# Moving the prologue and the last feed-forward of a two-layer sequence model: x first, tile 0 first, another order of steps

## The chip, the cores and the metric

One NeuronCore of a Trainium2 chip (trn2) runs the whole program in one launch. The metric is the device time in microseconds; lower is better. Engines are named as in the profile: PE (matrix products; PEld its weight loads), DVE (vector engine), ACT (activation functions), POOL (GpSimd) and SP (it issues most of the transfers). Every number is f32.

## The reference

The input x has 16 sequences of 512 tokens of 256 channels. Two layers follow each other, each an attention-like part and a feed-forward part, with a layer norm (LN, no weights) after each residual sum.

```
x = LN(x + attention(x))        # 16 heads of 16; q, k, v are taken on to 32 latents a head, rotary
                                # positions on q and k, a further matrix on q, causal softmax
x = LN(x + ffn(x))              # gate, up: 256 -> 704, down: 704 -> 256; silu(gate) * up;
                                # inputs AND weights of all three quantized to FP4 in blocks of 16
x = LN(x + recurrence(x))       # 16 heads with 64 states:
                                #   state[t] = tanh(state[t-1] @ tanh(a) + xnorm[t] @ b)
                                #   out[t] = state[t] @ c + skip * xnorm[t];   512 steps in order
x = LN(x + r * ((relu(k)**2) @ Wv))   # r = sigmoid(xr @ Wr), k = xk @ Wk; xr and xk mix each token
                                      # with the one before it
```

FP4 quantization takes the largest magnitude of each block of 16, scales by it and rounds to a grid of eight magnitudes. It needs a whole row of its input, and for the down projection a whole row of `h = silu(gate) * up`.

## The kernel before, in words

The program has two stages that follow each other. The first does layer 0 for one sequence after another; the second does layer 1 for all sequences at once, one time step after another. Between them layer 0's output goes to a DRAM tile `xs`, ordered by time and then by sequence.

**Prologue (lines 139 to 256).** Constants and weights are loaded on the queues of SP and ACT. The attention weights `caw` (768 KB) are transposed into `wqk`; the value, latent and output matrices are multiplied into each other (`there`, `wv`) and their biases into `bo`, which is added to the residual x. Only then do the pools for x open, and `load(0)` (line 709) asks for sequence 0's transposed x, `xT`. Then `heads`, `values` and the three steps of `latents` for head group 0 run, and the first scores can begin.

**Layer 0, main loop (lines 713 to 752).** A sequence has 4 groups of 4 heads, and each group has three slots (row blocks 3, 2, and 1 with 0). In a slot `scores` multiplies q and k (L551) into four PSUM banks, DVE adds the mask and takes the maximum (L563), `exponentials` runs on ACT (L576) two heads behind, and one slot later `turn` transposes the weights on PE (L586) and ACT copies them out (L588). After a group `weighted` multiplies by the values (L617), and `divide` divides by the sums (L638). Each slot is cut into 8 half slots. In a half slot the class `Beside` takes further steps from a list, so many that its planned times (`TIME`) are spread evenly over the sequence. The list is `PLAN`: a letter for the task, the sequence relative to the present one, and the tile or group. `H` are head products (L383), four steps; `V` values (L366); `L` latents, three steps (L401 with DVE at L411; L401, L416 and POOL at L417; L420 and ACT at L422); `O` the output projection with residual and LN (L435 to L448); `Q` starts a quantization; `U` gate and up (L483, L493), three steps; `D` down (L514, L524), two steps; `W` the feed-forward weights, 30 steps, in sequence 0 alone. So the feed-forward of sequence b runs beside the attention of b + 1 and b + 2. The order of PE is exactly the order in which the program is written down. A scheduler orders the other engines' queues. Quantizations (`fp4`, L290 to L304: eight operations on DVE, two on POOL) are cut into pieces, and `vector_step` writes down one piece in each half slot. PSUM has eight banks: one for `py`, seven that `mm` hands out. After the last sequence, `rest` runs what is left of the lists (lines 749 to 752): the output projection and the whole feed-forward of sequence 15, and the leftover tiles of sequence 14.

**Layer 1 (lines 755 to 1102).** Time step t multiplies the state (L988, `advance_state`), adds inputs that `inputs` (L950) has put into the PSUM tile `u` in groups of eight steps, and applies tanh on ACT (L996). Two halves of the heads alternate. Beside them run, in macro steps of 16 time steps, the tasks of layer 1's remaining work: `N` loads and RMS-normalizes tokens and transposes them (`normed`, L785 to L802), `R` reads the states out (L966), `A` is the product with `w_out`, `M` the token mixing, `K`, `G`, `V` the last feed-forward. `product` (L830) computes each of these products in two halves of 64 output columns. Two PSUM banks serve these tasks, three serve `u`. Macro step p needs the tokens 16p to 16p + 15 of all sequences, so the first eight need only tile 0 (tokens 0 to 127) of each.

Of the kernel before, what the change touches and what calls it, by code (L numbers as in the profile page):

```python
# [57 lines left out]
def tile_kernel(ctx: ExitStack, tc: tile.TileContext, I: dict, out: bass.AP):  # L58
# [79 lines left out]

    with ExitStack() as a:
        wts = a.enter_context(tc.tile_pool(name="wts", bufs=1))  # L140

# [23 lines left out]
        bd = {}  # L165
        for k in ("bdq", "bdk", "bdks"):
            bd[k] = wts.tile([P, 256], F32, name=k)
            nc.scalar.dma_start(bd[k], I[k])
# [14 lines left out]
        wgT = wts.tile([P, 2, FF], F32, name="wgT")  # L183
        wuT = wts.tile([P, 2, FF], F32, name="wuT")
        wdT = wts.tile([P, NFB, C], F32, name="wdT")
# [5 lines left out]
        with ExitStack() as s:  # L191
            prep = s.enter_context(tc.tile_pool(name="prep", bufs=1))
            pps = s.enter_context(tc.tile_pool(name="pps", bufs=4, space=PSUM))

            caw = prep.tile([P, 6, C], F32, name="caw")
            nc.sync.dma_start(caw, I["caw"].rearrange("(n p) c -> p n c", p=P))
            bdo = prep.tile([P, 256], F32, name="bdo")
            nc.scalar.dma_start(bdo, I["bdo"])
            rows = prep.tile([1, 512 + C], F32, name="rows")
            nc.sync.dma_start(rows, I["rows"])  # L200
            ones = prep.tile([P, P], F32, name="ones")
            nc.gpsimd.memset(ones, 1.0)


            for n in range(4):
                ps = pps.tile([P, 512], F32, tag="pp", name="ps_t")
                for cc in range(2):
                    nc.tensor.transpose(
                        ps[:, cc * P : cc * P + P], caw[:, n, cc * P : cc * P + P], ident
                    )  # L210
                to = wqk[:, :, n, :].rearrange("p c (h d) -> p c h d", h=2)
                of = ps[:, : 2 * P].rearrange("p (c h d) -> p c h d", c=2, h=2)
                for hf in range(2):
                    nc.any.tensor_copy(to[:, :, hf, :], of[:, :, 1 - hf if n > 1 else hf, :])

            turned = {}
            for k, t in (("k", bd["bdk"]), ("o", bdo)):
                turned[k] = prep.tile([P, 2, P], F32, name=f"turned_{k}")
                ps = pps.tile([P, 512], F32, tag="pp", name="ps_t")
                for cc in range(2):  # L220
                    nc.tensor.transpose(
                        ps[:, cc * P : cc * P + P], t[:, cc * P : cc * P + P], ident
                    )
                nc.any.tensor_copy(turned[k].rearrange("p c n -> p (c n)"), ps[:, : 2 * P])
            there = prep.tile([P, P], F32, name="there")
            ps = pps.tile([P, 512], F32, tag="pp", name="ps_g")
            for cc in range(2):
                nc.tensor.matmul(
                    ps[:, :P], turned["k"][:, cc, :], turned["o"][:, cc, :],
                    start=cc == 0, stop=cc == 1,  # L230
                )
            nc.any.tensor_copy(there, ps[:, :P])
            for cc in range(2):
                ps = pps.tile([P, 512], F32, tag="pp", name="ps_w")
                for hf in range(2):
                    nc.tensor.matmul(
                        ps[:, hf * P : hf * P + P], caw[:, 4 + hf, cc * P : cc * P + P], there,
# [31 lines left out]

        def fp4(dst, x, nb, rows=P):  # L270

# [918 lines left out]
```

## Time and profile before

| what | value |
|---|---|
| median of 3 runs | 2695.07 us (2691.79 to 2695.74) |
| the profiled execution, its own time | 2691.86 us |
| its span, first to last instruction | 2690.1 us |
| mean granted TensorE clock | 0.972 |
| PE busy | 2458.9 us (91%) |
| DVE busy | 1883.8 us (70%) |
| ACT busy | 1625.6 us (60%) |
| POOL busy | 1038.0 us (39%) |

Times are in microseconds from the first instruction unless marked ns. In a row of the profile `L551` is line 551 of the kernel before; `out<-in` names the tiles with buffer numbers left out; `xN` counts instructions. An f32 product appears as two PE instructions (passes). "idle before" is the time in which that engine stood idle just before, and after the arrow stands what ended it. PE's busy time is modelled for pipelined products, so a busy PE need not be at its peak. A queue name with q (SPq, ACTq) means that the engine only issues a transfer.

### The profile page before, as it was taken

Reading aid. Unit: us, or ns where it says so; the run is one execution under the profiler, and the core shown is the slowest. Engines: PE = TensorE matmul, PEld = TensorE weight load, DVE = VectorE, ACT = ScalarE, POOL = GpSimd, SP = SyncE. Lnnn points to the kernel's source line nnn. Section 1 sums busy time; section 2 is a strip of 40 time slices with the busy share of each in tenths; the row PEclk is TensorE's granted clock in tenths of the full one; section 3 lists DMA queues with packets and bytes.
Section 4 is the critical chain, followed back from the end, with each engine's and each line's share of the span. In section 5 each row is a group of like instructions: output and inputs, shape, how many; then the busy total and the mean of one; then the engine's idle time right before and its main releaser. Section 6 shows DMA issues by size and latency. Waiting matters only on the chain. (4 is left out here: it accounts for less than half of the span.)

```text
span 2690.1 us, 73796 instructions
## 1 busy us (share of the span) xinstructions
PE 2458.9 (91%) x28766; PEld 1707.3 (63%) x28766; DVE 1883.8 (70%) x5613; ACT 1625.6 (60%) x5604; POOL 1038.0 (39%) x1617
## 2 busy tenths in 40 slices
PE   6678999999999999999999999886699999999997
PEld 3445666666666666666666666564477777777775
DVE  3746878878788788787787877765456666666655
ACT  2646676666665756666666666561266666666663
POOL 4222323333233242332332323313445555555553
PEclk9879999999999999999999999997899999999998
DMA  3000000000000000000000000000101111111100
GB/s 119 23 9 11 5 23 13 15 23 13 13 21 7 23 13 13 23 9 19 13 15 23 13 6 15 5 7 6 42 27 38 38 38 36 36 38 38 34 27 21
DMA packets 58000, 61.31 MB, mean 23 GB/s; under 512 B 7857, under 2 KB 53041, under 8 KB 57650
## 3 DMA queue, kind: packets, MB, share of 16 engines
q1 hardware_dynamic: 56786, 55.54, 6.7%
q8 instruction: 226, 3.70, 0.6%
q10 hardware_dynamic: 864, 1.05, 0.1%
q14 instruction: 124, 1.02, 0.1%
HBM read 39.79 MB, written 16.78 MB: 21 GB/s over the span
## 5 line engine op out<-in xcount | busy, mean ns | idle before, releaser
L576 ACT ACTIVATE p<-p,nm 128x512 f32<-128x512 f32 (+3 forms) x1024 | 569.4, 561 | 491.7 <-DVE nm L563 486.4
L996 ACT ACTIVATE hist<-u 64x64 f32<-64x64 f32 x2048 | 444.2, 218 | 275.8 <-PE u L988 187.7
L563 DVE CUSTOM_DVE_ANT_0 p<-S,mask 128x512 f32<-128x512 f32 (+3 forms) x1024 | 443.1, 483 | 142.6 <-PE S L551 142.1
L586 PEld LDWEIGHTS ps_pt<-ident,p 128*128 128x128 f32 x2560 | 293.3, 142 | 248.8 <-issue 100.2
L988 PEld LDWEIGHTS u<-hist,ta 128*64 128x64 f32 x8176 | 360.0, 137 | 122.9 <-ACT hist L996 48.6
L586 PE MATMUL ps_pt<-ident,p 128*128 128x128 f32 x2560 | 398.2, 282 | 27.7 <-DVE qs L416 15.9
L588 ACT COPY pT<-ps_pt 128x384 f32<-128x384 f32 (+1 forms) x768 | 373.1, 514 | 80.4 <-PE ps_pt L586 80.1
L988 PE MATMUL u<-hist,ta 128*64 128x32 f32 x8176 | 391.2, 219 | 11.2 <-ACT hist L996 9.6
L303 POOL TENSOR_TENSOR q_q<-q_q,q_m 128x256 f32<-128x256 f32 (+1 forms) x142 | 167.2, 1177 | 595.4 <-DVE q_q L302 564.8
L551 PE MATMUL S<-kc,qr 32*128 32x512 f32 (+3 forms) x2048 | 221.4, 478 | 4.9 <-DVE qs L416 3.7
L950 PE MATMUL u<-xt,wb 128*64 128x64 f32 x4128 | 224.1, 231 | 0.9 <-DVE xt L802 0.6
L576 ACT ACTIVATION_READ_ACCUMULATOR p<-p,nm 128x1 f32 x1024 | 199.4, 195 | 0.0
L524 PE MATMUL ps_d<-wdT,hT 128*128 128x256 f32 (+1 forms) x768 | 195.7, 398 | 3.6 <-DVE kc L411 2.5
L82 POOL TENSOR_SCALAR ve<-mv 128x1 f32<-128x1 f32 (+2 forms) x144 | 28.6, 199 | 439.4 <-DVE mv L90 389.4
L493 PE MATMUL pg<-wgT,xqT 128*128 128x352 f32 x512 | 178.6, 472 | 6.8 <-DVE qc L411 6.6
L493 PE MATMUL pu<-wuT,xqT 128*128 128x352 f32 x512 | 174.1, 463 | 0.0
L524 PEld LDWEIGHTS ps_d<-wdT,hT 128*128 128x128 f32 (+1 forms) x768 | 140.7, 195 | 48.6 <-issue 24.7
L950 PEld LDWEIGHTS u<-xt,wb 128*64 128x64 f32 x4128 | 165.9, 139 | 6.6 <-DVE xt L802 1.1
L617 PEld LDWEIGHTS py<-pT,vpad 128*32 128x32 f32 x5120 | 140.0, 111 | 46.5 <-issue 24.4
L617 PE MATMUL py<-pT,vpad 128*32 128x128 f32 x5120 | 164.1, 277 | 4.5 <-ACT pT L588 4.2
L551 PEld LDWEIGHTS S<-kc,qr 32*128 32x128 f32 x2048 | 99.1, 186 | 76.3 <-issue 36.5
L1094 DVE COPY c<-hist 64x128 f32<-64x128 f32 x256 | 65.8, 257 | 97.7 <-ACT hist L996 92.3
(163 smaller groups left out, 4577.6 us busy)
## 6 DMA issues: line engine op xcount, KB each, us to landing
xT<-in_xT_dram SPq DMA_DIRECT2D x16, 512.0 KB
x<-in_x_dram SPq DMA_DIRECT2D x16, 512.0 KB
xs<-x SPq DMA_DIRECT2D x64, 128.0 KB
x<-xs SPq DMA_DIRECT2D x32, 256.0 KB
xm<-xs SPq DMA_DIRECT2D x32, 256.0 KB
out_dram<-o SPq DMA_DIRECT2D x64, 128.0 KB
caw<-in_caw_dram SPq DMA_DIRECT2D x1, 768.0 KB
w<-in_w_down_dram SPq DMA_DIRECT2D x2, 352.0 KB
```

The lines of the kernel that those rows point to most:

```text
L303: nc.gpsimd.tensor_tensor(q, q, m, ALU.subtract)
L493: nc.tensor.matmul(dst[:, :352], xqT[:, cc, :], w[:, cc, fs], start=cc == 0, stop=cc == 1)
L524: nc.tensor.matmul(ps[:, :C], hT[:n, kb, :], wdT[:n, kb, :], start=kb == 0, stop=kb == NFB - 1)
L551: nc.tensor.matmul(S[h][:, at : at + w], q[rs, i * P : i * P + P], k[rs, :w], start=True, stop=True,)
L563: nc.vector.tensor_tensor_reduce(out=p[:, own], in0=S[h][:, own], in1=mask[:, T - (i + 1) * P :], scale=1.0, scalar=-MASKED, op0=ALU.add, ...
L576: nc.scalar.activation(p[:, own], p[:, own], AF.Exp, bias=nm[:, u : u + 1], scale=-1.0, accum_out=sum_of[b, g][:, cb, half, h : h + 1],)
L586: nc.tensor.transpose(ps[:, at : at + P], p[:, at : at + P], ident)
L588: nc.scalar.copy(pT[:, :w], ps[:, :w])
L617: nc.tensor.matmul(py[q * 32 : q * 32 + 32, PLACE[i][1], :], vpad[b % 2][:, j, g * 4 + h, :], pt, start=j == 0 and h % 2 == 0, stop=j == i ...
L950: nc.tensor.matmul(u[rs, k, par:n:2, bs : bs + 16], wb[:, g * 2 + k, par, half, rs], xt[:, g, at : at + n - par : 2, :], start=par == 0 an ...
L988: nc.tensor.matmul(into[cs, :, c, :], ta[:, t % 2, g * 2 + k, cs], own[:, :, c, :], start=False, stop=True, skip_group_check=True,)
L996: nc.scalar.activation(state[g][rs, :, r * 32 : r * 32 + 32].rearrange("p k (s b) -> p k s b", s=2), u[rs, :, t - t0, :] .rearrange("p k ( ...
```

## The change

1. `caw` is split: the query and key rows (512 KB) are the second transfer on SP's queue and `xT` of sequence 0 the third; `bdq`, `bdk`, `bdks` come first on ACT's queue. The value rows (`cawv`) and the rest come behind.
2. The steps of the output weights (`output_weights`) are interleaved with two of the four head products and with group 0's latents of sequence 0. The values, the other two head products and the 30 weight steps of sequence 0 are spread over its half slots.
3. `heads` has one tile for groups 0 and 1 and one for groups 2 and 3; the second is computed in the sequence itself (`H0` in `PLAN`). `PLAN` has another order throughout.
4. The residual x has two buffers instead of three and is loaded at group 3 instead of group 0. The output projection normalizes two tiles at a time.
5. The pools of the feed-forward stay open beside layer 1. In the last sequence its list also holds the leftover steps of sequence 14. After it come the output projection of sequence 15 and a list `FIRST`: all four tiles' `U`, the down projection of tile 0 alone, and `N` of macro step 0 as soon as tile 0 is stored. The down projections of tiles 1, 2 (macro step 0) and 3 (macro step 1) are put beside the recurrence, in seven pieces each, in halves of 64 columns (`by_64`), with their copies on DVE.
6. PSUM: two banks stay with `mm` all along (`ps_2`), five more belong to layer 0 only and make room for `u` afterwards; `mm` takes the pools in turn.

```diff
+    ps_2 = ctx.enter_context(tc.tile_pool(name="ps_2", bufs=2, space=PSUM))
+    banks = [ps_2]
+
+    def mm(name):
+        banks.append(banks.pop(0))
+        return banks[-1].tile([P, 512], F32, tag="mm", name=name)
...
+    def by_64(dst, left, right, start, stop):
+
+        for c in range(2):
+            cs = slice(c * 64, c * 64 + 64)
+            nc.tensor.matmul(
+                dst[cs], left[:, cs], right, start=start, stop=stop, skip_group_check=True
+            )
...
+    def quantize_now(j):
+
+        for _ in quantize(B - 1, j):
+            vector_done(("x", B - 1, j))
...
+        ps = mm("ps_d")
+        for kb in range(NFB):
+            n = min(P, FF - kb * P)
+            product_of[0](ps[:, :C], hT[:n, kb, :], wdT[:n, kb, :], kb == 0, kb == NFB - 1)
+            if kb < NFB - 1:
+                yield 0.43, False
...
+        caw = wts.tile([P, 4, C], F32, name="caw")
+        nc.sync.dma_start(caw, I["caw"][: 4 * P].rearrange("(n p) c -> p n c", p=P))
...
+        load(0)
...
         def heads(b):
-            hs = heads_of[b] = att.tile([P, 4, T], F32, tag="heads", name="heads")
-            for n in range(4):
+            for n in (0, 2, 1, 3):
+                if n < 2:
+                    hs = heads_of[b, n] = att.tile([P, 2, T], F32, tag=f"heads{n}", name="heads")
...
         PLAN = [
-            "L0.1", "U-2.3", "U-2.3", "L0.1", "L0.2", "D-2.2", "O-1", "L0.1", "O-1", "Q-1.3",
-            "L0.3", "D-2.2", "Q-1.0", "V1", "L0.2", "V1", "D-2.3", "U-1.0", "L0.3", "L0.2", "D-2.3",
-            "Q-1.1", "U-1.1", "Q-1.2", "U-1.0", "U-1.0", "U-1.1", "H1", "H1", "D-1.0", "H1", "L0.3",
-            "U-1.2", "U-1.1", "U-1.3", "H1", "L1.0", "D-1.0", "D-1.1", "L1.0", "D-1.1", "L1.0",
-            "U-1.2", "U-1.2",
+            "L0.1", "L0.1", "U-2.3", "U-2.3", "H0", "H0", "O-1", "D-2.2", "L0.1", "D-2.2", "O-1",
+            "V1", "L0.2", "L0.2", "L0.3", "Q-1.0", "L0.3", "Q-1.1", "U-1.0", "L0.2", "D-2.3",
+            "U-1.1", "U-1.0", "U-1.0", "V1", "L0.3", "U-1.1", "Q-1.2", "H1", "U-1.2", "D-2.3",
+            "Q-1.3", "U-1.2", "U-1.1", "U-1.2", "H1", "U-1.3", "D-1.0", "D-1.0", "D-1.1", "L1.0",
+            "L1.0", "D-1.1", "L1.0",
         ]
...
-                if b == 0 and entry == "U-1.3":
-                    todo += [("W", ())] * 30
+            if b == B - 1:
+
+                todo += [(e[0], (b - 1, int(e[-1]))) for e in PLAN if e[1:3] == "-2"]
+            if b == 0:
+
+                todo[2:2] = [("V", (0,))] * 2
+                first = todo.index(("L", (0, 2))) + 3
+                n = len(todo) - first
+                for k in reversed(range(n)):
+                    at = first + k + 1
+                    todo[at:at] = [("W", ())] * ((k + 1) * 30 // n - k * 30 // n)
...
+            others = output_weights()
+            for name, args in [("H", (0,))] * 2 + [("L", (0, 0))] * 3:
+                step(name, args)
+                next(others, None)
...
+                    if g == 3 and n == 0:
+                        load_residual(b)
...
-            beside.rest()
-            for b in (B, B + 1):
-                Beside(b).rest()
+            last_projection = out_projection(B - 1)
+            next(last_projection)
+            quantize_now(0)
+            next(last_projection)
...
+    FIRST = [
+        "E3", "U0", "U0", "E1", "U0", "U3", "U1", "U1", "D0", "E2", "F0", "D0", "U1", "U2", "N0",
+        "U2", "U3", "F1", "U2", "N0", "F2", "U3",
+    ]
+    LATER = {
+        0: [
+            *[("D", 1)] * 7, *[("D", 2)] * 7,
+        ],
+        1: [
+            *[("D", 3)] * 7,
+        ],
+    }
...
-        for _ in normed(0):
-            pass
+        for e in FIRST:
+            end = False
+            while not end:
+                step(e[0], int(e[1:]))
+                end = ends[0]
+        banks[:] = [ps_2]
+        five.close()
+        ps_u = ctx.enter_context(tc.tile_pool(name="ps_u", bufs=3, space=PSUM))
+
+        copier[0] = nc.vector.tensor_copy
+        product_of[0] = by_64
```

In `FIRST` the letter E is a quantization of one x tile at once, F the end of one of `h`. `output_weights` holds the same transposes and products as the prologue before (lines 216 to 256), cut into four pieces. `ffn_up`, `ffn_down`, `fp4` and `ffn_weights` keep their operations and move in front of the attention's pools.

## The prediction

> **What bounds the kernel now.** I read first the page's forty slices, then the engines' busy time by stretch, and only where those showed PE short of work, the timeline. The page's two rows (each digit a tenth of one fortieth of the span, 67.3 us):
>
> ```profile
> PE   6678999999999999999999999886699999999997
> ...
> PEclk9879999999999999999999999997899999999998
> ```
>
> PE is full except at three places: the first four slices, slices 26 to 29, and the end. Busy time by stretch (start:end, length, then PE, PEld, DVE, ACT, POOL busy with counts, granted clock, DMA share, GB/s):
>
> ```profile
> 120.00:140.00 20.00, 8.49 (x33) 4.95 (x34) 14.09 (x35) 11.25 (x39) 8.25 (x7) 0.55 0.00 1
> 608.30:717.10 108.80, 105.12 (x853) 68.67 (x852) 87.08 (x267) 71.76 (x218) 36.47 (x42) 1.00 0.05 16
> 1695.60:1804.20 108.60, 90.78 (x757) 60.54 (x757) 78.16 (x238) 59.51 (x185) 30.74 (x36) 0.92 0.02 6
> 1860.00:1880.00 20.00, 9.29 (x31) 6.56 (x32) 8.69 (x15) 2.06 (x6) 7.40 (x6) 0.67 0.02 7
> 2000.00:2100.00 100.00, 95.88 (x2084) 77.02 (x2082) 59.20 (x164) 64.03 (x291) 58.32 (x125) 1.00 0.14 40
> ```
>
> Row 2 is one whole sequence in mid-run: PE is idle 3.7 of 108.8 us, so no new order of steps can give much more than that for each of them. Row 3 is the last sequence, row 4 the feed-forward that is left behind it: half empty, at two thirds of the clock. Row 5 is the recurrence, full. The two thin places in the timeline (start, us, engine, line, operation), first the start, then the way from attention to recurrence:
>
> ```profile
> 25.18 0.39 SPq L351 DMA_DIRECT2D xT<-in_xT_dram  x1
> 29.08 9.20 PE L383 MATMUL ps_h<-xT,wqk 128*128 128x512 f32 x16 [3.98 <-DMA xT<-in_xT_dram]
> 48.61 2.09 PE L551 MATMUL S<-kc,qr 32*128 32x512 f32 x8 [0.87 <-ACT qr L422]
> ```
> ```profile
> 1819.73 0.88 DVE L638 TENSOR_TENSOR yT<-py,rT 64x256 f32<-64x256 f32 x2 [1.80 <-ACT rT L633]
> 1836.14 1.38 DVE L448 TENSOR_SCALAR x<-x,mv,rstd 128x256 f32<-128x256 f32 x4 [3.42 <-POOL rstd L84]
> 1916.71 1.01 DVE L96 TENSOR_SCALAR x<-x,mv,rstd 128x256 f32<-128x256 f32 x1 [2.66 <-POOL rstd L84]
> 1919.78 0.88 SPq L785 DMA_DIRECT2D x<-xs  x2
> 1927.72 3.84 PE L950 MATMUL u<-xt,wb 128*64 128x64 f32 x72 [0.65 <-DVE xt L802]
> 1929.87 0.45 ACT L996 ACTIVATE hist<-u 64x64 f32<-64x64 f32 x2 [19.75 <-PE u L950]
> ```
>
> The first scores stand at 48.6 us; the x that they need is asked for at 25.2. The last attention output is divided at 1820.6 and the recurrence's first tanh is at 1929.9: 109.3 us in which PE has only feed-forward tiles, each waiting for its own quantization. First scores of each sequence, read off the timeline: 48.6, 166.3, 282.9, then every 108.7, the last at 1695.6.
>
> **The change, part by part.**
>
> (1) *x first.* xT of sequence 0 goes from behind some twenty transfers on SP's queue (25.2) to third, behind cols and a caw cut to 512 KB. xT took 3.9 us (25.18 to 29.08) and caw 7 us amid others (4.58 to 11.65); together, with bdq, bdk, bdks beside them on ACT's queue, I put caw at 6 and xT at 8 to 9. Then: eight transposes 1.9 and their copies 0.9 (to 9); two of four head products 4.6 (half of 9.20); a head's activation 0.9; latents of group 0 from 41.7 to 48.6, 6.9; that is 22 if nothing lay between. But the order on PE puts the output weights' steps between these, 10 us of PE work in before (13.8 to 25, with waits), of which the gaps of the latents' chain (DVE and POOL, some 4 us) hide part; and each waits for its own transfer (bdo and cawv now come later), in front of the next head product. I add 9: first scores at 31, bounds 26 and 38. **Gain 17.6** (10 to 22).
>
> (2) *Sequence 0* (117.7 us). It takes on values (3.6 of PE) and two head products (3.9), and loses its bunched weight steps: between 75 and 166 PE waited 27 us, 21 of it for them (9.2, 6.4 and 5.6 in the chain of waits), at a clock down to 0.55. Spread over three quarters of the sequence they have some 6 us each, against 2.4 us of DVE and 1.3 of POOL for a tile. But ACT's tanh of ta now stands behind the first four exponentials and waits for all eight ta loads, and these stand behind six more transfers on SP: 0 to 8, I take 2. Thin sequences also run at a lower clock (row 3). 21 − 7.5 − 2 − 2 for new small waits: **gain 10** (0 to 18). Sequence 1 (116.6), with the same thin filling and 12 us of PE waits, **gain 3** (−3 to 8).
>
> (3) *Step order, heads in two tiles*, sequences 2 to 14. The waits to be removed:
>
> ```profile
> PE ps_pt L586 <- DVE qs L416: 3.7, 3, 1.2
> PE ps_q L401 <- DVE nm L563: 2.3, 3, 0.8
> PE pg L493 <- DVE qc L411: 1.7, 3, 0.6
> ```
>
> (over three sequences). They come from one thing: the latents of group 3 start 8.2 us of planned time before those of group 2 are done with the single qc buffer, and hold one of seven PSUM banks from 633.5 to 656.7. In the new order it is 2 us of planned time. I take 2 of the 3.7. Against it: the last latent step of the next sequence's group 0 is now the very last filler, where before 4.8 us of feed-forward (planned) lay behind it; then come ACT's 0.69 for qr and a hand-off, against 0.45 of transposes: 1 us of wait in front of each sequence's first scores. Two more rstd pairs on POOL (0.2 and 0.55) go unseen in its 72 idle us. Residual x with two buffers: its load waits for the second-last sequence's last store (1.8) and lands 4.3 later, and POOL's four adds (2.8) wait at the head of POOL's queue; behind them stand quantizations of the next tile, due some 10 us later by the plan, and none before; in before POOL stood idle 6.2 us at the same place, unseen. Uncovered it would be 9 us. Net 0.7 a sequence (−2.5 to 3.7): **gain 9** (−30 to 48).
>
> (4) *Last sequence.* Before: 125 us from first scores (1695.6) to divided output (1820.6), some 12 more than a regular sequence and the same drain. Now the pace is a regular one's, since the five leftover steps of sequence 14 are in its list: PE 12.7 us of work that lay behind. I take 118: **gain 7** (0 to 13).
>
> (5) *The way to the recurrence.* The old 109.3 becomes a chain through tile 0. From the divided output, with rows of before: projection half 1.8, add and statistics 1.6, rstd 0.8, two normalizations 0.8, hand-offs 1: 6. Quantize x: DVE 2.4 plus 1.5 of the other half's statistics; POOL 1.3, behind four memsets of the history (0.95 each, half hidden): to 12. Transposes, copy, 0.9 and hand-offs: 13.3; four products at 1.18: 18; tanh and two DVE steps: 19.5. fp4 of h: DVE 4.5 alone, 7 with what stands between in DVE's order; POOL 1.67 + 1.38: to 29.6. PE has only 3 us for this wait of 11: clock down. Down projection with transposes, copy, 12 passes at row 4's clock: 35; add, norm: 38. From there as before, 1916.7+1.0 to 1929.9, 12.2: store, load, RMS, transposes, u. One U step (2.4) stands before u on PE: 52. The other U steps fill the waits. **Gain 57** (48 to 64).
>
> Rule against row here: the Trainium skill, "TensorE: Matmul & The Clock Gate", part 1, says that PE falls to half clock after an idle window of about 3.4 us and needs as long to come back. That speaks against this part: its three long waits would cost some 1.7 us each, 5 in all. Row 4 shows 0.67 granted amid such waits. My 35 holds 2 us of it already, as the down projections in this stage took 3.8 to 4.7 us against 2.95; by the rule the gain would be 54. I take the rows.
>
> (6) *Three down projections beside the recurrence.* Macro steps (16 time steps) 0 and 1 took 18.4 and 23.8 us, a full one 22.8. In halves of 64 columns:
>
> ```profile
> L524 PE MATMUL ps_d<-wdT,hT 128*128 128x256 f32 (+1 forms) x768 | 195.7, 398 | 3.6 <-DVE kc L411 2.5
> ...
> L834 PE MATMUL ps_kv<-wvT,ka 128*64 128x256 f32 x512 | 80.3, 395 | 0.0
> ```
>
> 195.7/768 is 0.255 a pass; 80.3/512 is 0.157. By the skill's "TensorEngine Tiling (Array Packing)", theoretical speedup, two 64-column tiles run up to twice as fast, so that halves cost nothing: 24 × 0.1275 = 3.06, like 12 × 0.255. By the row it is 24 × 0.157 = 3.8. I take the row; with transposes 4.6 for each. A full step adds 12.3 us of such work to the bare 15.5 and takes 7.3 longer: 0.6 of it shows. So 0.6 × 13.8: **loss 8** (4 to 14). Its copies move to DVE, which is at 59 of 100 there. Stores of tiles 1 to 3 stand in SP's queue before later loads, but are first needed 8 macro steps on.
>
> Sum: 17.6 + 10 + 3 + 9 + 7 + 57 − 8 = 95.6 from the profiled span of 2690.1: 2594.5. That run took 2691.9, 1.8 more than its span, and the median of the runs is 3.2 above it: **2600 us**.
>
> **Rivals.** *A, the step order clears nearly all of the waits*: 3.2 a sequence instead of 0.7, 33 us less: 2567. For it: the bank held for 23 us. Against it: waits for nm and hq are not of that cause. *B, tile 0's chain stays serial and cold*: each long wait costs twice what I took and sequence 0 gains nothing; 20 + 10 + 5: 2635. For it: row 4. *C, tile 0 finishes early but the u products wait for banks*, that is, the tail change does not do what it says, since the last U steps hold the same space: tail gain 40, 2617; inside the main range. *D, slower*: the late last latent. PE stands at each sequence's first scores until qr is there; if ACT reaches qr only behind a queue of exponentials, masks and exponentials restart from empty. Price: ACT's queue of four exponentials and two copies (0.75 each) and a slot's restart, up to 8 us; it decides from 95.6/15 = 6.4 a sequence. At 8: 2720. Against it: ACT is idle a third of each sequence.
>
> **How the numbers follow.** Main sum (with C) 0.66, A 0.14, B 0.16, D 0.04. A measurement of this kernel tells about 0.2% (5 us) from nothing. Only D ends above: faster 0.95, same 0.01, slower 0.04. Half-widths added in squares (7, 9, 5, 18, 6, 8, 5) give about 25; with A and B taken in: 2558 to 2640.
>
> **What would show it.** First scores at 26 to 38; distance of first scores in mid-run 106 to 110; from the divided output to the first tanh 48 to 60; macro steps 0 and 1 at some 24 and 27. Wrong, if mid-run distances leave 105 to 111, since 13 of them count, or if the tail stays above 70.

## The result, and the profile after

The changed kernel takes 2657.21 us (median of 4 runs, 2655.69 to 2659.3) where the kernel before, measured beside it, took 2694.66 (2691.79 to 2695.74): a ratio of 0.9863, 95% interval 0.9846 to 0.988. It is faster, but by 37 us (1.4%) and not by 95, and its time lies above the range of 2558 to 2640. The profiled execution has a span of 2655.9 us (before 2690.1). Its busy and clock rows, each digit one fortieth of the span (66.4 us); in all rows from here on, `L527` is line 527 of the kernel that ran, whose lines are numbered otherwise than those of the kernel before:

```profile
PE   7788999999999999999999999976899999999997
...
PEclk9898999999999999999999999987899999999999
```

The hole between the layers has shrunk from slices 26 to 29 to slices 27 to 29. Busy time by stretch (start:end, length, PE, PEld, DVE, ACT, POOL busy with counts, granted clock, DMA share, GB/s):

```profile
587.80:697.20 109.40, 106.56 (x848) 70.17 (x849) 88.69 (x267) 71.26 (x217) 37.20 (x44) 1.00 0.05 16
1675.00:1819.50 144.50, 125.21 (x964) 84.09 (x965) 93.99 (x285) 74.41 (x223) 39.35 (x48) 0.91 0.03 11
1819.50:1840.00 20.50, 9.84 (x29) 6.30 (x28) 14.65 (x41) 0.84 (x2) 9.89 (x16) 0.67 0.00 1
1840.00:1875.40 35.40, 25.16 (x126) 16.06 (x125) 26.59 (x60) 5.17 (x13) 14.35 (x16) 0.90 0.13 41
1875.40:1906.40 31.00, 26.32 (x479) 21.36 (x475) 16.80 (x43) 14.02 (x65) 22.02 (x35) 0.83 0.13 40
1906.40:1937.60 31.20, 26.39 (x461) 20.44 (x458) 13.59 (x38) 13.97 (x65) 11.51 (x28) 0.78 0.09 24
```

Row 1 is a mid-run sequence: PE is busy 97% of it, and it is no shorter than the 108.8 us of before. Row 2 is the last sequence, with 19.3 us in which PE is idle. Rows 3 and 4 are the way from the divided output to the recurrence's first tanh, rows 5 and 6 are macro steps 0 and 1, at a clock of 0.8. Three places of the timeline that bound the stages, the first scores, the last divided output and the first tanh (start, us, engine, line, operation):

```profile
32.52 1.24 PE L527 MATMUL S<-kc,qr 32*128 32x512 f32 x4 [0.87 <-ACT qr L481]
...
1818.66 0.88 DVE L614 TENSOR_TENSOR yT<-py,rT 64x256 f32<-64x256 f32 x2 [3.05 <-ACT rT L609]
...
1875.42 0.45 ACT L1062 ACTIVATE hist<-u 64x64 f32<-64x64 f32 x2 [4.43 <-PE u L1016]
```

With the starts of the sequences' first scores and of the recurrence's steps read off both traces, each part of the prediction has its own measurement (us of the span):

| stage | before | after | predicted gain | measured gain |
|---|---|---|---|---|
| (1) up to the first scores | 48.6 | 32.5 | 17.6 | 16.1 |
| (2) sequence 0 | 117.6 | 104.3 | 10 | 13.3 |
| (2) sequence 1 | 116.6 | 124.7 | 3 | **−8.1** |
| (3) sequences 2 to 14 | 1412.7 | 1413.5 | 9 | **−0.8** |
| (4) last sequence, to its divided output | 125.0 | 144.5 | 7 | **−19.5** |
| (5) divided output to first tanh | 109.3 | 55.9 | 57 | 53.4 |
| (6) macro steps 0 and 1 | 42.2 | 62.2 | −8 | **−20.0** |
| the rest of the recurrence | 718.0 | 718.3 | 0 | −0.3 |
| sum | 2690.1 | 2655.9 | 95.6 | 34.2 |

The two large gains, and that of sequence 0, came as worked out. Four others failed, and the experiments are about these.

Each experiment's time is that of a single run, unless a median is named, so effects are read from the stage that was changed and not from the whole. In the runs below that leave a stage's code as the change left it, that stage repeats as follows: first scores at 30.8 to 32.5 us, sequence 0 in 103 to 107, sequence 1 in 124.7 to 125.8, sequences 2 to 14 in 108.6 to 108.9 each, the last in 142 to 146, the rest of the recurrence in 715 to 723. Differences of this size are not read as effects.

### The profile page after: what moved, and what is told of

The parts are those of the page before. It is cut to its first block, busy times and chain, and to the rows that moved or that the text cites. A ratio compares the mean times of both kernels' runs of the same rounds, so it can differ in the third digit from the quotient of the medians.

```text
span 2655.9 us, 73932 instructions
## 1 busy us (share of the span) xinstructions
PE 2480.2 (93%) x28802; PEld 1724.5 (65%) x28802; DVE 1926.2 (73%) x5624; ACT 1616.4 (61%) x5593; POOL 1050.6 (40%) x1649
## 4 chain that ended last, share of the span: by engine, by line
PE 62%; DVE 24%; ACT 6%; issue 3%; POOL 3%; DMA 1%; SPq 1%; ACTq 0%; POOLq 0%; DVEq 0%
PE ps_pt L562 7%; PE u L1054 7%; PE S L527 6%; PE ps_d L158 5%; PE pg L158 4%; PE pu L158 4%; PE py L593 4%; PE u L1016 4%; DVE p L539 3%; PE ps_h L442 3%; ACT p L552 3%; PE ps_a L900 2%; PE ps_k L900 2%; PE ps_rr L900 2%; PE ps_kv L900 2%
## 5 line engine op out<-in xcount | busy, mean ns | idle before, releaser
L527 PE MATMUL S<-kc,qr 32*128 32x512 f32 (+3 forms) x2048 | 238.2, 475 | 11.6 <-ACT qr L481 9.5
L158 PE MATMUL ps_d<-wdT,hT 128*128 128x256 f32 x732 | 192.9, 408 | 7.3 <-ACT hT L323 6.0
L476 POOL TENSOR_TENSOR qc<-qc,qs 128x512 f32<-128x512 f32 x64 | 81.5, 1274 | 231.2 <-DVE qs L475 216.3
L158 PEld LDWEIGHTS ps_d<-wdT,hT 128*128 128x128 f32 x732 | 136.5, 200 | 47.8 <-issue 16.2
L527 PEld LDWEIGHTS S<-kc,qr 32*128 32x128 f32 x2048 | 110.3, 184 | 79.4 <-issue 40.4
L82 POOL TENSOR_SCALAR ve<-mv 128x2 f32<-128x2 f32 (+1 forms) x160 | 30.7, 192 | 322.1 <-DVE mv L90 318.1
```

Of the source, the lines that this page charges most:

```text
L158: nc.tensor.matmul(dst, left, right, start=start, stop=stop)
L527: nc.tensor.matmul(S[h][:, at : at + w], q[rs, i * P : i * P + P], k[rs, :w], start=True, stop=True,)
```

## The experiments

**The last sequence: a list with holes.** In the last sequence the entries that belong to sequence 16 (head products, values, latents) drop out of `PLAN`, and the six leftover steps of sequence 14 are put at its end. The table of waits shows what PE waited for between 1675 and 1820. The first name is the product that stood waiting, behind the arrow stands what it waited for, then the us in total, the times and the longest; `xq` and `hq` are quantized rows of x and h, `hT` is `hq` transposed, and `ps_` marks a PSUM tile:

```profile
PE ps_xq L286 <- POOL xq L213: 7.2, 1, 7.2
PE ps_h L321 <- POOL hq L213: 3.6, 1, 3.6
PE ps_d L158 <- ACT hT L323: 3.2, 1, 3.2
```

Two of the three are quantizations. The same stretch in the kernel before, without the leftover steps, was

```profile
1695.60:1820.60 125.00, 105.34 (x907) 70.94 (x907) 89.53 (x274) 71.39 (x223) 33.77 (x39) 0.93 0.02 5
```

PE was idle for 19.7 us there, and for 19.3 after the change: the leftover steps came on top of the idle time and did not fill it. `q15` writes the same steps in another order, with each quantization further ahead of its reader and the leftover steps among the others:

```diff
-                todo += [(e[0], (b - 1, int(e[-1]))) for e in PLAN if e[1:3] == "-2"]
+                last = (
+                    "L15.1 L15.1 U13.3 U13.3 H15 H15 O14 D13.2 L15.1 D13.2 O14 Q14.0 Q14.1 L15.2 L15.2 U14.0 "
+                    "D13.3 L15.2 U14.1 U14.0 L15.3 U14.0 L15.3 Q14.2 Q14.3 U14.1 D13.3 L15.3 U14.2 U14.1 U14.3 "
+                    "D14.0 U14.2 D14.0 U14.2 D14.1 U14.3 U14.3 D14.1 D14.2 D14.2 D14.3 D14.3"
+                ).split()
+                todo = [(e[0], tuple(map(int, e[1:].split(".")))) for e in last]
```

> Only the list of the last sequence is written anew: the same 42 steps, but each quantization is started some five steps ahead of the tile that reads it, and the leftover steps of sequence 14 stand between the others, not behind them. After the change this sequence took 144.5 us from its first scores (1675.0) to its divided output (1819.5), with 19.3 us in which PE was idle. Theory 1 (the steps of sequence 16 that drop out of this list, head products, values and latents, were the cover of the quantizations; without them PE waits for xq and hq and then runs at half clock): 144.5 falls to 125 to 132, the waits at ps_xq and ps_h of 7.2 and 3.6 us are gone, and the whole falls by 12 to 19 us to some 2640. Theory 2 (the last sequence is longer only because it holds 12.7 us more of PE work): 144.5 stays within 3.

2639.55 us. The last sequence, by stretch and by waits:

```profile
1673.20:1800.60 127.40, 117.49 (x964) 78.32 (x965) 93.49 (x285) 73.64 (x223) 40.51 (x48) 0.99 0.04 13
```
```profile
PE ps_xq L286 <- POOL xq L213: 2.7, 1, 2.7
PE ps_d L158 <- ACT hT L323: 1.8, 1, 1.8
```

The same 964 instructions take 127.4 us in place of 144.5. Of these 17.1 us, 9.4 are idle time (19.3 to 9.9) and 7.7 are PE's busy time, which fell from 125.2 to 117.5 as the granted clock went from 0.91 to 0.99. So theory 1 holds in its time: the sequence was long for its waits and for the lower clock behind them. The wait for `hq` is gone, that for `xq` is down from 7.2 to 2.7. Two things remain open. `q15` moves the quantizations and the leftover steps together, and no run separates the two. And it shows that the order matters, not that the missing steps of sequence 16 are the reason: that part of theory 1 is argued. What is left above a regular sequence, 127.4 − 108.7 = 19, contains the drain and the leftover work.

`q15_tail` takes one of the leftover down projections (`D14.3 D14.3`) out of that list and puts it behind the first half of the output projection:

```diff
             quantize_now(0)
+            step("D", (B - 2, 3))
+            step("D", (B - 2, 3))
             next(last_projection)
```

> The run q15 with one of the leftover down projections (sequence 14, tile 3) taken out of the last sequence's list and put behind the first half of the output projection, where PE waited 10.2 us for xq. Theory 1 (this wait is free cover): the last sequence falls by 2.5 to 3.5 us from 127.4, the way from the divided output to the first tanh (54.0) grows by no more than 1. Theory 2 (the residual sum and the norm behind this down projection stand in DVE's way, which makes xq): the way grows by 2 to 4 us, and nothing is won.

2637.0 us. The last sequence went from 127.4 to 129.1, the way to the first tanh from 54.0 to 52.5. The sum, 181.4 to 181.6, is unchanged: nothing is won, as theory 2 had it, but neither theory's numbers came. The sequence did not get shorter with less work in it, and the way did not get longer with more.

**Macro steps 0 and 1: the work or its place?** `order` gives these two macro steps another order and changes nothing else:

```diff
-        return todo + LATER.get(M, [])
+        if M == 0:
+            return (
+                [("N", 1), ("N", 2)] + [("D", 1)] * 5 + [("N", 1)] + [("D", 1)] * 2
+                + [("D", 2)] * 7 + [("N", 2)]
+            )
+        if M == 1:
+            return (
+                [("N", 3), ("R", 0)] + [("D", 3)] * 2 + [("A", 0)] * 4
+                + [("D", 3)] * 5 + [("M", 0), ("N", 3)]
+            )
+        return todo
```

> Only macro steps 0 and 1 get another order: the norm of the next tokens has seven down-projection pieces between its first and second step, and in macro step 1 the pieces of tile 3 stand between the product with w_out and the token mixing. Macro steps 0 and 1 took 30.95 and 31.21 us after the change (18.4 and 23.75 before). Theory 1 (stalls: the second step of the norm waits up to 1.8 us for POOL, the mixing up to 3.2 us for DVE, and half clock follows each): the two together fall from 62.2 to 50 to 55 us, the whole by 7 to 12. Theory 2 (the down projections themselves, PE's work and the copies on DVE, cost this much): 60 or more.

2645.59 us; macro steps 0 and 1 took 26.35 and 24.42, together 50.8: theory 1. In the changed kernel PE's two longest waits in these steps were (`xn` are the tokens that `N` has normalized, `x` the sum that `A` has normalized and `M` transposes)

```profile
PE ps_x L879 <- DVE x L887: 3.9, 2, 3.2
PE ps_xn L879 <- POOL xn L863: 3.2, 3, 1.8
```

and 13.5 us at half clock lay around the wait of 3.2, which ended at 1918.6:

```profile
1917.50:1931.00 13.50, 11.22 (x118) 8.54 (x120) 8.40 (x21) 3.49 (x16) 6.08 (x12) 0.50 0.02 6
```

With the other order neither wait is there (two others, of 2.2 and 1.6 in total, are), and the two steps by stretch are

```profile
1875.60:1901.95 26.35, 23.61 (x478) 19.28 (x474) 16.95 (x38) 13.94 (x64) 20.38 (x31) 0.94 0.13 38
1901.95:1926.37 24.42, 22.38 (x462) 17.98 (x459) 12.29 (x36) 13.93 (x64) 11.26 (x26) 0.93 0.12 35
```

The clock rose from 0.83 and 0.78 to 0.94 and 0.93. 50.8 against 42.2 before leaves 8.6 us for the three down projections: the 8 of the prediction. The other 11.4 are 4.7 of PE's idle time (9.5 to 4.8) and 6.7 of its busy time (52.7 to 46.0, for 940 instructions in both), at a lower clock. They go back to two places, `N`'s second step right behind its first, and `M` right behind `A`. At the first, DVE and POOL are still at the quantizations of h: `lessdve` (below), which shortens these and keeps the order, takes 24.1 us for macro step 0, with a clock of 1.00, and 31.3 for macro step 1.

`whole` computes these down projections in one piece (the line `product_of[0] = by_64` is left out).

> Only the down projections beside the recurrence are computed in one piece of 128 columns in place of two of 64: 36 products fewer in macro steps 0 and 1. Theory 1 (the measured rows: 24 passes of 0.157 us against 12 of 0.255): 0.7 us less for each of three tiles, macro steps 0 and 1 fall by 1 to 3 us. Theory 2 (a half of 64 columns runs twice as fast beside its twin, so that halves cost nothing): within 0.5 us. Theory 3 (longer passes stand in the way of the recurrence's own products): 2 us or more slower.

2657.52 us, and macro steps 0 and 1 took 65.1 in place of 62.2: the number of theory 3. All of it lies in macro step 1 (34.1 for 31.2; step 0 took 31.0 in both), where the clock was 0.75 in place of 0.78; how much is longer passes in the recurrence's way and how much the clock is not shown. The groups of the down projection in the two steps, first of the changed kernel, then of `whole` (count, busy us, mean ns, idle before):

```profile
L164 PE MATMUL ps_d<-wdT,hT 128*64 128x256 f32 (+1 forms) x72 | 12.9, 441 | 0.0
```
```profile
L158 PE MATMUL ps_d<-wdT,hT 128*128 128x256 f32 (+1 forms) x36 | 14.1, 478 | 0.0
```

Here 72 halves cost 4.3 us a tile and 36 whole ones 4.7. The prediction had 3.8 for halves by one row and 3.06 for whole ones by another; the second row, from layer 0, did not carry over to this place. The Trainium skill's "TensorEngine Tiling (Array Packing)", theoretical speedup, gives a speedup of up to 2 where a dimension is 64 or less, so that halves would cost no more than whole ones: it was the nearer guide to the comparison.

**Sequence 1: the other list with holes.** In sequence 1 the entries of sequence −1 drop out, ten microseconds of planned time, most of it at the front of the list. `pause1` puts nine of planned time without instructions in their place:

```diff
                 c = b + int(c)
+                if c < 0 and b == 1 and entry[0] in "UD":
+                    todo += [("P", (b,))] * 3
                 if 0 <= c < B:
```

> The changed kernel, with pauses (planned time without an instruction) in sequence 1's list where the steps of sequence -1 drop out of it. Sequence 1 took 124.7 us after the change, 116.6 before and 116.7 with the old order. Theory 1 (as in the last sequence: where steps drop out of the list, the rest move together, and the quantizations and the output projection come before what they wait for): 124.7 falls to 112 to 119. Theory 2 (the loss of sequence 1 comes from sequence 0's late work, the weights and loads): it stays above 122.

2648.32 us. Sequence 1 took 111.6 us: theory 1. (The whole fell by less than these 13 us, since sequence 0 and the rest of the recurrence took 2.4 and 3.2 longer, within what their unchanged code varies by.) Its longest waits after the change, and then with the pauses (`nm` is a row block's maximum, which DVE takes from the scores, `xqT` the transposed `xq`):

```profile
PE pg L158 <- DVE nm L539: 3.2, 1, 3.2
PE pg L158 <- ACT xqT L288: 3.2, 1, 3.2
PE ps_d L158 <- ACT hT L323: 2.6, 1, 2.6
PE ps_o L494 <- DVE yT L614: 2.6, 1, 2.6
```
```profile
PE ps_pt L562 <- DVE nm L539: 3.2, 3, 1.2
PE pg L158 <- ACT xqT L288: 1.9, 1, 1.9
```

Empty time made the sequence 13 us shorter: the steps behind it no longer crowd ahead of what they wait for. The same entries were missing before the change, when the sequence took 116.6 us, so the holes alone do not make the loss: it is the new order with the holes. The old order gives 116.7 in the changed kernel (`oldorder`, below), the new one without the holes 111.6.

**Mid-run: why did nothing come?** Two runs undo parts of (3) of the change; two more were meant to move a part of (4).

> The changed kernel with its step order, but the heads of a sequence in one tile again, as before the change, not in two. Theory 1 (the two tiles matter, since the next sequence's head products must not write over heads that the last latents still read): sequences 2 to 14 rise by 0.5 to 3 us each. Theory 2 (the step order already keeps them apart): within 0.3 of 108.7.

`onetile` (heads in one tile, written by all four products) took 2658.91 us, sequences 2 to 14 on average 108.7: the two tiles make no difference under the new order.

> The changed kernel, with one thing moved: the four additions of the bias to the residual x on POOL come two slots after x is asked for, not at once, so that they no longer wait 6.1 us for the transfer at the head of POOL's queue in each sequence. Theory 1 (this wait is covered, as the prediction had it as likeliest): sequences 2 to 14 stay within 0.4 us of 108.7. Theory 2 (it holds up quantizations and eats what the step order brought): they fall by 1 to 4 us each, the whole by 13 to 50.

`lateadd` (the additions written down in slot 2 of group 3 in place of slot 0) took 2654.89 us, 108.7 a sequence, but it moved nothing. A scheduler orders POOL's queue, and the additions stand in it where they stood, with the same wait. One sequence of the changed kernel, then of `lateadd`:

```profile
1103.18 2.79 POOL L415 TENSOR_TENSOR x<-x,bo 128x256 f32<-128x256 f32 x4 [6.20 <-DMA x<-in_x_dram]
1111.56 1.69 POOL L212 TENSOR_TENSOR q_q<-q_q,q_m 128x704 f32<-128x704 f32 x1 [5.58 <-DVE q_q L211]
```
```profile
1101.10 2.80 POOL L418 TENSOR_TENSOR x<-x,bo 128x256 f32<-128x256 f32 x4 [6.17 <-DMA x<-in_x_dram]
```

So this run is the changed kernel once more and decides nothing. The rows of the changed kernel do: behind the additions POOL stands idle again, for 4.0 to 5.6 us in each of the sequences 2 to 14, until DVE has the next quantization ready for it. The wait for x holds up nothing on POOL, as the prediction had it.

> The step order of before is put back for all sequences, with the two head products of the sequence's own groups 2 and 3 as its fourth and fifth step, since the heads stay in two tiles. All else is as changed. Theory 1 (the new order itself gained nothing in mid-run, since PE's waits went from the fillers into the scores): sequences 2 to 14 stay at 108.5 to 109.5 us, and PE's idle time goes back to 3 us or more a sequence. Theory 2 (the new order gained its 0.7 us or more and something else of the change, such as the residual loaded at group 3, took it away): sequences 2 to 14 rise to 109.5 or more. For sequence 1 (124.7 us after, 116.6 before): if the new order is its cause it falls to 115 to 119, if the weight steps and loads are, it stays above 122.

`oldorder` took 2816.47 us. Sequences 2 to 14 rose to 120.2: theory 2 in its direction, but far more than the 0.7 that it was about. Sequence 1 fell to 116.7, so there the new order is the cause. In one of sequences 2 to 14:

```profile
PE ps_h L321 <- POOL hq L213: 4.5, 2, 4.4
PE ps_pt L562 <- DVE nm L539: 3.9, 1, 3.9
```

> The old step order in the changed kernel, with the same additions moved as in the run lateadd. With the old order alone sequences 2 to 14 took 119.9 us on average, with waits of 4.4 us for hq (behind POOL's 6.3 us wait for x) and 3.9 us for DVE in each. Theory 1 (the residual's new place and its wait at the head of POOL's queue is what the old order cannot bear): they fall by 4 to 8 us each. Theory 2 (the two head products moved into the sequence are what the old order cannot bear): they stay within 1.5 us of 119.9.

`oldorder_lateadd` took 2816.07 us, 120.2 over the 13 sequences. The additions stayed where they were here too, so this is `oldorder` once more. Its trace speaks against theory 1 all the same: behind the additions POOL is idle for 3.7 to 4.4 us in each of these sequences, until DVE has the next quantization ready. What remains is the two head products, now at places 4 and 5 and gone from the middle of the list, the two-tile norms and the new pools of banks; which of these was not tried, nor was the old order with the heads in one tile. So the new order does matter: with the other edits it is 11.5 us a sequence better than the old one, and the sum of all is nil.

The next three move single steps, to take away waits of the changed kernel. There PE's waits look small, but the table hides two. A group of scores is 8 or 16 PE instructions on four PSUM banks; most groups take 0.93 to 1.14 us from first to last, but in each sequence one takes 2.52 and one 1.88, because products within it wait for a bank. This counts as busy. Before the change the two longest took 2.04 and 1.47. Over sequences 2 to 14 PE's idle time fell from 3.6 to 2.1 us a sequence and its busy time rose by 1.6, of which 1.3 is in the score groups (13.5 to 14.9 us a sequence).

> The changed kernel with two small moves in the step list: the second U step of tile 1 one place ahead of the second V and the last L0.3 step, and the last D step of tile 1 behind the latents of the next group. After the change two score groups a sequence take 2.5 and 1.9 us in place of 0.93, as they wait for a PSUM bank that DVE releases late (the gate and up products stand close before them), and the first scores wait 0.54 for qr. Theory 1 (these 3 us are a loss that can be had back by the order alone): sequences 2 to 14 fall from 108.7 to 106 to 107.7. Theory 2 (PE's waits go elsewhere, since DVE and POOL set the pace): within 0.6 of 108.7.

```diff
-"U-1.0", "U-1.0", "V1", "L0.3", "U-1.1", "Q-1.2", "H1",
+"U-1.0", "U-1.0", "U-1.1", "V1", "L0.3", "Q-1.2", "H1",
...
-"D-1.0", "D-1.0", "D-1.1", "L1.0", "L1.0", "D-1.1", "L1.0",
+"D-1.0", "D-1.0", "L1.0", "D-1.1", "L1.0", "L1.0", "D-1.1",
```

2741.33 us, 114.8 a sequence. The score group of 2.52 us took 0.93, and in its place came the wait in the second line below; the third step of the latents, no longer behind a down projection, waited for POOL and DVE (first line), and one score group took 3.33 with a wait of 0.7:

```profile
PE ps_qf L479 <- POOL qc L476: 2.7, 1, 2.7
PE ps_xq L286 <- POOL xq L213: 1.5, 1, 1.5
PE S L527 <- DVE qc L470: 0.7, 1, 0.7
```

> The changed kernel with the quantization Q of tile 2 and the second U step of tile 1 both moved ahead of the second V and the last L0.3 step; the latents of the next group stay where the change put them. In the run mid the U step's move took the score group at bank wait from 2.5 to 0.93 us, but PE then waited 1.5 us for xq of tile 2, and the moved D step cost 5 us a sequence behind it. Theory 1 (each wait is the distance of one chain from its reader, and can be had back by giving both their distance): sequences 2 to 14 fall from 108.7 to 106.5 to 107.7. Theory 2 (DVE, busy 80% in these sequences, sets the pace, and a wait taken from one place comes up at another): within 0.6 of 108.7, or slower.

> As mid2, and also the first latents step of the next sequence's group 0 one D step earlier, so that its vector work lies between two D steps and not right ahead of the last score group (which took 1.9 us in place of 0.93). Theory 1: 0.5 to 1 us less than mid2 for each of sequences 2 to 14. Theory 2: the same as mid2 within 0.4, or slower.

`mid2` (`Q-1.2` moved ahead too; the tail of the list as in the changed kernel) took 2658.98 us, 108.8 a sequence. `mid3` took 2658.13, 108.9, its waits in one sequence being

```profile
PE ps_d L158 <- DVE nm L539: 1.7, 1, 1.7
PE ps_xq L286 <- POOL xq L213: 1.5, 1, 1.5
```

In `mid3` both long score groups are gone (0.93 each): 1.59 and 0.95 us were taken away there, and 1.5 and 1.7 appeared elsewhere. Over sequences 2 to 14 the score groups fell from 14.9 to 12.3 us a sequence and PE's idle time rose from 2.1 to 4.7: the same 2.6. Theory 2, twice. `lessdve` then takes work from DVE:

> The changed kernel without two of the eight DVE operations of each quantization (the exponent mask and the scaling of it, together 1.0 us for a row block of h and 0.6 for one of x), so that nothing is rounded to the FP4 grid and the output differs; all other operations stay. That takes some 6.4 us of DVE's 88 in each sequence. Theory 1 (DVE, which is busy 13.8 of the 14.1 us before the score group that waits 1.6 us for a bank, sets the pace there): sequences 2 to 14 fall from 108.7 by 1.5 to 3. Theory 2 (PE's own work sets it, and waits and busy time only trade places): less than 0.6.

```diff
-        nc.vector.tensor_scalar(m.bitcast(U32), q.bitcast(U32), 0x7F800000, None, ALU.bitwise_and)
-        nc.vector.tensor_scalar(m, m, 1.0, 1.5 * 2.0**22, ALU.max, ALU.mult)
-        nc.vector.tensor_tensor(q, q, m, ALU.add)
-        nc.gpsimd.tensor_tensor(q, q, m, ALU.subtract)
+        nc.vector.tensor_tensor(m, q, q, ALU.add)
+        nc.gpsimd.tensor_tensor(q, m, q, ALU.subtract)
```

2628.31 us, 107.3 a sequence, 1.4 less: between the theories, near the first. A sequence of it, and the like one of the changed kernel:

```profile
1008.30:1114.80 106.50, 105.06 (x852) 69.06 (x852) 82.62 (x251) 71.65 (x217) 36.80 (x44) 1.00 0.05 16
```
```profile
1023.50:1131.60 108.10, 106.44 (x848) 70.19 (x849) 88.65 (x267) 71.12 (x217) 37.19 (x44) 1.00 0.05 16
```

DVE's work fell by 6.0 us, PE's busy time by 1.4 and its idle time by 0.2. The gain is in the score groups: the two long ones took 1.97 and 0.94 in place of 2.52 and 1.88. So 6 us less work on DVE are worth 1.4 us of 108.7 here, and PE stays busy for some 105.

> The changed kernel with one operation of each quantization of h (the product with the inverse scale, 0.88 us on DVE, 704 elements a row) on POOL, which is busy 34% of these sequences; some 3.5 us of DVE's 88 go, and 6 us come to POOL. Theory 1 (DVE sets the pace): sequences 2 to 14 fall by 0.5 to 2 each. Theory 2 (PE sets it): within 0.6. Theory 3 (POOL's operation is 1.5 us long, lies in the chain from h to hq, and DVE's short operations beside a POOL operation took 1.4 to 1.6 us in place of 0.2 to 0.3): sequences rise by 1 to 6.

`pool` (one line: the product with the inverse scale on `nc.gpsimd` for rows of 704) took 2701.24 us, 111.9 a sequence, 3.1 more: theory 3's number; how its two reasons share in it was not tried.

**All three repairs together.** `allthree` is the changed kernel with the edits of `q15_tail` (which holds that of `q15`), `order` and `pause1`.

> The changed kernel with what q15_tail, order and pause1 changed, together. If the three losses are separate, their gains add: sequence 1 at 112, sequence 15 at 129, the first tanh 53 after the divided output, macro steps 0 and 1 at 51 together; from the changed kernel's span of 2655.9 that is 13 + 18.5 + 11.4 less and up to 2 more for sequence 0, or 2615 us, 3.0% below the kernel before. If they hang together (a shifted start of a stage brings back a wait), 2622 to 2640.

2612.24 us, median of 5 runs (2611.23 to 2613.51), against 2695.82 for the kernel before: ratio 0.9691, interval 0.9678 to 0.9705. The rows of its page:

```profile
PE   7798999999999999999999999987899999999997
...
PEclk9899999999999999999999999997999999999999
```

The gains add, each within 3 us: sequence 1 took 108.8 us (112 expected), the last 131.0 (129), the way to the first tanh 53.2 (53), macro steps 0 and 1 50.6 (51). The sum had said 2615.

## Why the prediction was wrong, by its own steps

Of the 95.6 us that the sum promised, 34.2 came. Of the 61 that are missing, 59 lie in four terms: 26.5 in (4), 12.0 in (6), 11.1 in sequence 1 of (2), 9.8 in (3).

- **(1) x first: right.** 31 predicted, 32.5 measured. The 9 us put down for the output weights are a lump that no run takes apart.
- **(2) Sequence 0: right** (10, measured 13.3). **Sequence 1: wrong**, outside its −3 to 8. The step was costed by likeness to sequence 0, without writing down which entries of the list exist in sequence 1. `oldorder` and `pause1` show the new order over these holes as the cause.
- **(3) Step order: the waits went, the gain did not come.** "The waits to be removed", `ps_pt <- DVE qs`, `ps_q <- DVE nm` and `pg <- DVE qc`, are no longer among PE's waits in sequences 2 to 14. The step that failed is to count them as time won. What PE's idle time lost (1.5 us a sequence) its busy time gained (1.6), most of it inside the score groups, where the table of waits does not show it, and moving single steps only moved it on (`mid2`, `mid3`). The small terms stood: POOL's wait for the residual is covered (its idle time behind the additions shows it), and the late last latent costs 0.54 us a sequence, where 1 was taken.
- **(4) Last sequence: the largest miss.** "Now the pace is a regular one's, since the five leftover steps of sequence 14 are in its list" (they are six). The 118 is as much as PE's busy time of before, 105.3, and the 12.7 of leftover work. It has nothing for the 19.7 us in which PE was idle there: the leftover steps were taken to fill these. They did not, 19.3 us of idle time stayed, and PE's busy time rose by 19.9 at a clock of 0.91 in place of 0.93. With another order (`q15`) PE's busy time was 117.5, as the 118 had it, and 9.9 us of idle time were left: 127.4. A likely reason for the idle time is that a regular list has seven more steps (two `H`, two `V`, three `L`), which stand between its quantizations and their readers; no run shows this by itself.
- **(5) The way to the recurrence: right**, 53.4 for 57. By the Trainium skill's "TensorE: Matmul & The Clock Gate", part 1, the prediction had worked out 54 and had set it aside. The clock in this stage was 0.67 in its first 20 us and 0.90 in the rest; no run separates the 3 us between the two.
- **(6) Down projections: the mechanism right, one term missing.** The work costs 8.6 (`order`), 8 was predicted. Missing were the 11.4 us of waits, and of slow clock behind them, at the steps that the new pieces stand beside: only the pieces were costed, not the order of `N`, `A` and `M` around them, nor the quantizations that DVE and POOL still had to do there.

What the range missed: four of the six parts share one kind of cost, a chain through DVE and POOL that lost its distance from its reader. The misses fell in one direction, and adding half-widths in squares treated them as independent. It also took 18 as the half-width of (3), whose bounds of −30 and 48 are 39 from their middle; with 39 the root is 42 in place of 25, and 2657 would still have been outside. Rival B came nearest in its number, by waits that cost twice, but in other stages than its own; A, C and D did not happen. Of the signs that were to show the prediction right, three came (first scores at 32.5, 108.7 in mid-run, 55.9 to the first tanh) and the macro steps did not. None of them looked at sequence 1 or at the last one, where 38 of the 61 us were lost.

## What to carry to other kernels

When a list of steps is reused where some of its entries do not exist (first, second, last iteration), write that shortened list out and look at the distance of each producer on DVE or POOL from its reader: the missing steps may have been cover. When you add work to a stage with idle time, do not take the idle time as filled before you know what it waits for. Sum busy and idle time before you believe that a wait is gone, as a wait for a bank within a group of products counts as busy. And cost a moved piece of work together with the neighbours it separates or brings together.

## What was not expected of the hardware

In the 14.1 us up to the end of the long score group DVE is busy for 13.8, and two of its short operations take several times their length (timeline of the changed kernel):

```profile
1084.84 1.68 POOL L212 TENSOR_TENSOR q_q<-q_q,q_m 128x704 f32<-128x704 f32 x1 [0.90 <-DVE q_q L211]
1084.95 1.59 DVE L202 TENSOR_SCALAR q_inv<-q_inv 128x16 f32<-128x16 f32 x1
...
1086.59 1.66 POOL L213 TENSOR_TENSOR hq<-q_q,q_sc 128x704 f32<-128x704 f32 x1
1087.04 1.36 DVE L207 TENSOR_SCALAR q_m<-q_q 128x256 uint32<-128x256 uint32 x1
1088.44 0.29 DVE L208 TENSOR_SCALAR q_m<-q_m 128x256 f32<-128x256 f32 x1
...
1089.11 0.51 DVE L303 SCALAR_TENSOR_TENSOR th<-th,pg 128x352 f32<-128x352 f32 x1
...
1089.67 0.18 PEld L527 LDWEIGHTS S<-kc,qr 32*128 32x128 f32 x1 [0.56 <-DVE th L303]
```

In sequences 2 to 14 the operation of L202 on 16 elements took a median of 1.59 us in the 13 cases that began beside a POOL operation and 0.17 in the 39 others; that of L207 on 256 elements 1.36 and 0.28. In the rows above each ends within 0.15 us after the POOL operation beside it. Not every operation of DVE is held: the reduction of L199 over 256 elements took 0.41 in all 52 cases, 13 of which began beside a POOL operation. The Trainium skill's "SBUF — State Buffer", section "SBUF: two separate sides", has GpSimd and certain operations of DVE share a port pair that one of them holds for a whole instruction; these rows agree. The operation of L303 reads the gate product out of its bank, and the last row has the next scores waiting for just that. That these 2.5 us of blocked DVE time are what makes it late is argued from the order of the lines, not shown by a run of its own.
